# One transformer block with adaptive layer norm: shift matmuls first, reciprocals on ScalarE, last bias in the partial sums

## The chip, the core and the metric

The kernel runs on one core of one Trainium2 chip. A core has TensorE (PE), which multiplies matrices into PSUM; VectorE (DVE), ScalarE (ACT) and GpSimd (POOL), which work element by element; and SyncE (SP), whose queue here issues nearly all of the DMAs. ScalarE looks functions such as exponential or gelu up in tables that come in sets; a function from another set needs a table load first. The metric is the time of one execution on the device, in microseconds (us), lower is better. The time of a kernel is the median of its runs.

## The reference

A block over x of shape 8 x 1024 x 512, float32, with 16 heads of 32 columns and a hidden width of 2048. Weights, biases and the condition are inputs.

```python
mod = silu(condition) @ Wada + bada
sh_a, sc_a, gt_a, sh_m, sc_m, gt_m = split(mod, 6, axis=1)
xn = layernorm(x, g1, be1)
xm = xn * (1.0 + sc_a[:, None, :]) + sh_a[:, None, :]
x = x + gt_a[:, None, :] * attention(xm, Wqkv, Wproj, bproj)   # causal softmax
xn = layernorm(x, g2, be2)
xm = xn * (1.0 + sc_m[:, None, :]) + sh_m[:, None, :]
h = gelu(xm @ W1 + b1)
x = x + gt_m[:, None, :] * (h @ W2 + b2)
```

## The kernel before

The 8 x 1024 rows are cut into 16 blocks of 512 rows; a batch element has two. A block n goes through normalization, transposes, the three projections q, k and v, attention, the output projection, a second normalization, and the two matrix products around the gelu. The attention of block n runs while the projections of the next block and the products of the block before it are done, so that TensorE always has a second stream of work.

The linear products (helper `matmul`, L197) use TensorE as 128 rows x 32 columns: four matmuls stand side by side, one for each strip of 32 columns, and make one set. The attention works on 32 rows x 128 columns: four heads of 32 side by side. Transposes (L641) use all of 128 x 128. The kernel's own planner calls these "columns", "rows" and "whole" (`note_pe`) and charges 150 ns where one follows another. float32 products are run by the chip as two passes, so one matmul of the program is two records of the trace; bf16 takes one. Products of halves of matrices are combined in the manner of Strassen: sums of weight quarters are prepared once and kept in DRAM (`kept_up_S` and the like), and partial sums u1, u2, u3, u5, v3 are combined as they leave PSUM.

Attention has two kinds of tile, both in one PSUM buffer of four banks, `st`, which there is only once. A score tile (`scores_at_once`, L1391) has q as weights and k moving; VectorE adds the causal mask (L1405) and takes the maxima of rows (L1408). The maxima are split into three bf16 parts (`split_maxima`), turned into a row by TensorE (L1446) and copied out by ScalarE as `mrow` (L1452). A weight tile (`weights_T`, L1461) has k as weights (L1472) and then, in the same PSUM accumulation, a shift: minus ones times the row of maxima, in bf16 (L1484). ScalarE's exponential makes `pT` out of it (L1496), GpSimd cuts away what lies above the diagonal (L1501) and adds up the tiles of a group for the denominators (L1614), and `weigh` multiplies with v (L1524). A tile holds one part of 512 columns, or parts of 384 and 128, or two of 256.

`finish` (L1534) closes a group of four heads: TensorE sums the denominators (L1545), ScalarE copies them to `rec` (L1554) and the weighted sums to `top` (L1557), VectorE inverts `rec` in four pieces (L1563), which are put among its other work as jobs, and GpSimd multiplies (L1588).

`normalize` and `normalize_tile` take mean and variance on VectorE, the root on ScalarE (L563, L599) and its reciprocal on VectorE (L565, L604). `gates` makes the rows that scale the two residual sums: ga and gm, and gba and gbm, which are the gate times the bias (bproj, b2). `down` (L990) begins by adding gbm to the residual, a tile of 128 rows at a time (L1075), and copies its first partial sum u1 out of PSUM (L1079).

The order on every engine is written out by the program itself: a planner keeps a clock for each engine (`now`), the time at which each buffer is written and free (`written`, `left`), and costs that it notes with each instruction. `step_aside` (L1252) puts linear work ahead of an attention tile until the tile's inputs are due, the row of maxima among them; `work` takes the thread whose wait is the shortest; `either` (L150) gives an element-wise operation to VectorE or GpSimd, `copy_out` (L181) to VectorE or ScalarE. So an edit that changes a cost moves instructions elsewhere.

Of the kernel before, what the change touches and what calls it, by code (L numbers as in the profile page):

```python
# [22 lines left out]
def kernel(  # L23
# [259 lines left out]
    GATES = {"a": (2, bproj), "m": (5, b2)}  # L283
# [78 lines left out]
    vecs = [(g1, NC), (be1, NC), (g2, NC), (be2, NC), (bproj, NC), (b2, NC), (b1, NF), (bada, NMOD)]  # L362
# [7 lines left out]
    O_G1, O_BE1, O_G2, O_BE2, O_BPROJ, O_B2, O_B1, O_BADA = at  # L370
# [24 lines left out]
    nc.gpsimd.memset(minus_ones, -1.0)  # L395
    mcols = const.tile([P, NTT, P], BF16, tag="mcols", name="mcols")
# [7 lines left out]
    warm = const.tile([P, 1], F32, tag="warm", name="warm")  # L404
    nc.scalar.activation(warm, eps, AF.Sqrt)
    table[0] = "sqrt"
# [53 lines left out]
    def gates(kind):  # L460

        i, bias = GATES[kind]
        at = take(4)
        part = {kf: halves(j) for kf, j in zip(RAW, at)}
        b_gate = tmp.tile([P, D], F32, tag="y", name=f"b_gate_{kind}")[:B, :]
        b_out = tmp.tile([P, D], F32, tag="y", name=f"b_out_{kind}")[:B, :]
        nc.sync.dma_start(b_gate, bada[i * D : (i + 1) * D].unsqueeze(0).to_broadcast([B, D]))
        nc.sync.dma_start(b_out, bias.unsqueeze(0).to_broadcast([B, D]))
# [12 lines left out]
        release(*at)  # L481
        combine_out(b_gate, bank, ps, b_gate)
        nc.vector.tensor_tensor(b_out, b_out, b_gate, ALU.mult)
        note("DVE", 700, port=True)
        for name, row in ((f"g{kind}", b_gate), (f"gb{kind}", b_out)):
            kept_rows[name] = kept.tile([B, D], F32, tag=f"kept_{name}", name=f"kept_{name}")
            nc.sync.dma_start(kept_rows[name], row)

    def gate_broadcasts(b, kind):

        for name in (f"g{kind}", f"gb{kind}"):
# [52 lines left out]
    def normalize(tiles, key, sources):  # L544
# [17 lines left out]
        def root():  # L562
            nc.scalar.activation(rstd, mv[:, :, 1], AF.Sqrt, bias=eps)  # L563
# [26 lines left out]
    def normalize_tile(xt, key, t, source):  # L590
# [8 lines left out]
        nc.scalar.activation(rstd, mv[:, 1:2], AF.Sqrt, bias=eps)  # L599
        note_act(300, "sqrt", [("mv", key, t)], [("rstd", key, t)])  # L600
        written["hat", key, t] = NEVER

        def apply():
            nc.vector.reciprocal(rstd, rstd)  # L604
# [3 lines left out]
            nc.scalar.activation(xh, xt, AF.Identity, bias=offset, scale=rstd)  # L608
            note_act(800, None, [("rstd", key, t)], [("hat", key, t)])
            hats.setdefault(key, []).append(xh)  # L610
# [275 lines left out]
    def add_to(xt, other, reads, writes, op=ALU.add):  # L886
        either(xt, xt, other, op, [*reads, *writes], writes)
# [102 lines left out]
    def down(n, part):  # L990
# [81 lines left out]
        if part == 0:  # L1072
            yield [("g", n, 0), ("g", n, 1), "prepared"], []
            for i in range(NTT):
                add_to(residual[n][:, i, :], gate_rows["gbm"], [("row", "gbm")], [("xr", n, i)])  # L1075
# [3 lines left out]
            copy_out(got["u1"], bank, ps, [key("u1")])  # L1079
# [16 lines left out]
        elif part == 2:  # L1096
# [5 lines left out]
            settle(n, 0, 1, v3, key("v3"))  # L1102
        else:
# [357 lines left out]
    def weights_T(n, g, parts):  # L1461
# [6 lines left out]
        for k, c0, w, gg in parts:  # L1468
            kT = keys_of(n, k // NTT)
            for j in range(HPG):  # L1470
                r = slice(j * hd, (j + 1) * hd)
                nc.tensor.matmul(  # L1472
                    st[:, j, c0 : c0 + w],
                    kT[r, gg, ts(k % NTT, P)],
                    qT[r, gg, TB - w :],
                    start=(c0 == 0),
                    stop=False,
                    skip_group_check=True,
                )
        for k, c0, w, gg in parts:  # L1480
            row = m_rows[n, gg]
            for j in range(HPG):
                r = slice(j * hd, (j + 1) * hd)
                nc.tensor.matmul(  # L1484
                    st[:, j, c0 : c0 + w],
                    minus_ones[r, :],
                    row[r, TB - w :],
# [7 lines left out]
        used = parts[-1][1] + parts[-1][2]  # L1495
        nc.scalar.activation(pT[:, :, :used], st[:, :, :used], AF.Exp, scale=scale)  # L1496
# [37 lines left out]
    def finish(n, g):  # L1534
# [19 lines left out]
        nc.scalar.copy(rec, banks[bank])  # L1554
        note_act(585, None, [("l", bank)], [kr])
# [3 lines left out]
        part = TB // 4  # L1559

        def invert(i):
            some = rec[:, i * part : (i + 1) * part]
            nc.vector.reciprocal(some, some)  # L1563
            note("DVE", 920, [kr], [kr])

        if (n, g) == groups[-1]:
            for i in range(NTT):
                invert(i)
                some = slice(i * part, (i + 1) * part)
# [4 lines left out]
        if (n, g) == first_end:  # L1574
            for i in range(NTT):
                invert(i)
# [5 lines left out]
        def quotient():  # L1582
            invert(3)
            if n == NB - 1 and g == NC - 2:
                nc.vector.tensor_tensor(qTs[n][:, g, :], top, rec, ALU.mult)
                note("DVE", 700, [kr, "top"], [("att", n)], port=True)
            else:
                nc.gpsimd.tensor_tensor(qTs[n][:, g, :], top, rec, ALU.mult)  # L1588
                note("POOL", 1285, [kr, "top"], [("att", n)])
            if g == NC - 1:  # L1590
                written["attended", n] = 0.0
# [197 lines left out]
```

## Time and profile before

| | |
|---|---|
| median of 3 runs | 3600.94 us (3596.26 to 3602.02) |
| span of the profiled execution | 3594.6 us |
| TensorE busy | 98% |
| VectorE, ScalarE, GpSimd busy | 58%, 37%, 57% |
| mean granted clock of TensorE | 0.998 |

The profile is of one execution. Its page gives the busy time of each engine, the chain of waits that ended last, and the costliest groups of instructions. Views of the same trace list instructions in order of time, or group them by line, or list who waited for whom. In a group, `out<-in` are buffer names, then come partitions x elements and type, the count, the busy time, the mean length of one in ns, and the idle time before them with what ended it. "PE" is a matmul, "PEld" a load of weights. A line such as "PE sc L1391 <- DVE mx L1408: 8.1, 8, 1.1" says that TensorE waited for VectorE 8.1 us in total, 8 times, at most 1.1 us. A row of the windows view has the stretch, its length, then busy time and count of PE, PEld, DVE, ACT and POOL, the granted clock, the DMA engines' busy share and the GB/s that they moved.

### The profile page before, as it was taken

The numbers are of one execution on the slowest core, as the hardware profiler recorded it, in microseconds if no ns is written. First come the engines' busy times: TensorE is split into PE (matmuls) and PEld (weight loads), VectorE is DVE, ScalarE is ACT, GpSimd is POOL, SyncE is SP. The second block draws the span as 40 slices with busy tenths as digits, with TensorE's granted clock in tenths as the row PEclk, the third lists the DMA queues.
The fourth block names the chain that finished last, engine by engine and source line by source line (L and its number), as shares of the span: only waits on it lengthen the run. The fifth ranks groups of instructions, "written<-read, shape, count | busy, mean of one in ns | idle before, by whom it ended". The sixth has DMA issues, their size and how long they took to land.

```text
span 3594.6 us, 121150 instructions
## 1 busy us (share of the span) xinstructions
PE 3529.1 (98%) x54845; PEld 1774.2 (49%) x54845; DVE 2073.7 (58%) x2296; ACT 1328.0 (37%) x1395; POOL 2045.4 (57%) x2176
## 2 busy tenths in 40 slices
PE   8999999999999999999999999999999999999999
PEld 4444455445554555545555455444554545445445
DVE  6766675554746556465564655646557355564663
ACT  2335233352433524335242452424524244241421
POOL 3676746565465753666536665466654566544660
PEclk9999999999999999999999999999999999999999
DMA  6743233434343343433434334343343433335334
GB/s 201 235 150 90 81 116 104 121 104 130 110 125 104 105 132 113 142 93 99 128 112 137 98 99 128 109 131 104 98 131 104 139 99 105 121 95 154 90 113 137
DMA packets 307893, 430.34 MB, mean 120 GB/s; under 512 B 25900, under 2 KB 176236, under 8 KB 307380
## 3 DMA queue, kind: packets, MB, share of 16 engines
q1 hardware_dynamic: 307264, 422.56, 38.6%
q8 instruction: 432, 7.08, 0.8%
q14 instruction: 81, 0.66, 0.1%
q10 hardware_dynamic: 116, 0.03, 0.0%
HBM read 394.12 MB, written 28.38 MB: 118 GB/s over the span
## 4 chain that ended last, share of the span: by engine, by line
PE 89%; DVE 5%; POOL 3%; ACT 2%; issue 1%; DMA 1%; SPq 0%; ACTq 0%; DVEq 0%; POOLq 0%
PE bank L201 62%; PE sc L1391 8%; PE st L1472 8%; PE po L1524 7%; DVE mx L1408 2%; PE st L1484 2%; PE bank L1545 2%; PE bank L641 1%; POOL pT L1614 1%; ACT pT L1496 1%; DMA w<-in_L_cond_Wada_dram 1%; POOL xr L161 1%; DVE xr L158 0%; PE bank L1446 0%; DVE hT L1005 0%
## 5 line engine op out<-in xcount | busy, mean ns | idle before, releaser
L1614 POOL TENSOR_TENSOR pT<-pT,pT 128x256 f32<-128x256 f32 (+3 forms) x1254 | 1188.1, 983 | 430.6 <-PE po L1524 241.4
L1496 ACT ACTIVATE pT<-st 128x2048 f32<-128x2048 f32 x288 | 541.0, 1879 | 874.2 <-PE st L1484 832.5
L201 PE MATMUL bank<-w,hT 128*32 128x256 f32 x14336 | 807.5, 380 | 1.2 <-ACT rec L1554 0.9
L1408 DVE TENSOR_REDUCE mx<-sc 128x4 f32<-128x2048 f32 (+3 forms) x383 | 663.5, 1753 | 165.5 <-PE sc L1391 159.5
L201 PEld LDWEIGHTS bank<-w,hT 128*32 128x32 f32 x14336 | 454.8, 110 | 346.3 <-issue 54.2
L201 PE MATMUL bank<-xm_m,w 128*32 128x256 f32 x8192 | 496.0, 380 | 3.2 <-ACT xm_m L651 3.0
L201 PE MATMUL bank<-t_m,w 128*32 128x256 f32 x6144 | 388.7, 381 | 0.5 <-DVE t_m L660 0.5
L1501 POOL TENSOR_SCALAR_AFFINE_SELECT pT<-pT 128x512 f32<-128x512 f32 x256 | 165.4, 665 | 390.4 <-ACT pT L1496 390.4
L201 PEld LDWEIGHTS bank<-xm_m,w 128*32 128x32 f32 x8192 | 255.4, 110 | 225.9 <-issue 58.6
L1391 PE MATMUL sc<-kT,qT 32*128 32x512 f32 (+3 forms) x3064 | 328.0, 520 | 8.7 <-DVE mx L1408 8.1
L1472 PE MATMUL st<-qT,kT 32*128 32x512 f32 (+3 forms) x3072 | 329.9, 520 | 6.6 <-DVE mx L1408 5.3
L1405 DVE TENSOR_TENSOR sc<-sc,mask 128x1024 f32<-128x1024 f32 (+1 forms) x159 | 162.1, 1020 | 281.8 <-PE sc L1391 272.0
L1524 PE MATMUL po<-pT,v 128*32 128x512 f32 (+3 forms) x3072 | 304.2, 491 | 8.6 <-POOL pT L1501 8.6
L201 PEld LDWEIGHTS bank<-t_m,w 128*32 128x32 f32 x6144 | 188.3, 110 | 192.0 <-issue 75.5
L201 PE MATMUL bank<-xm_a,w 128*32 128x256 f32 x3968 | 240.3, 380 | 0.9 <-ACT p_k L188 0.9
L201 PE MATMUL bank<-w,qT 128*32 128x512 f32 x2048 | 237.4, 594 | 0.0
L1563 DVE RECIPROCAL rec<-rec 128x128 f32<-128x128 f32 x256 | 225.7, 920 | 11.3 <-ACT rec L1554 11.3
L1391 PEld LDWEIGHTS sc<-kT,qT 32*128 32x128 f32 x3064 | 129.6, 183 | 177.8 <-ACT pT L1496 78.9
L1472 PEld LDWEIGHTS st<-qT,kT 32*128 32x128 f32 x3072 | 129.8, 183 | 165.8 <-issue 72.6
L193 DVE TENSOR_TENSOR hT<-bank,u_u 128x512 f32<-128x512 f32 x192 | 129.0, 685 | 104.8 <-PE bank L201 104.1
L201 PE MATMUL bank<-t_a,w 128*32 128x256 f32 x2944 | 188.3, 380 | 0.0
L1427 POOL CAST mcols<-mx 128x16 bf16<-128x16 f32 x61 | 15.6, 256 | 289.9 <-DVE mx L1422 157.0
(206 smaller groups left out, 3608.6 us busy)
## 6 DMA issues: line engine op xcount, KB each, us to landing
w<-in_L_cond_W_dram SPq DMA_DIRECT2D x384, 256.0 KB
w<-kept_up_S SPq DMA_DIRECT2D x256, 256.0 KB
w<-kept_down_S SPq DMA_DIRECT2D x256, 256.0 KB
w<-kept_qkv_S SPq DMA_DIRECT2D x180, 256.0 KB
w<-in_L_cond_Wqkv_dram SPq DMA_DIRECT2D x147, 256.0 KB
hat<-in_x_dram SPq DMA_DIRECT2D x64, 256.0 KB
w<-in_L_cond_Wproj_dram SPq DMA_DIRECT2D x64, 256.0 KB
xr<-in_x_dram SPq DMA_DIRECT2D x64, 256.0 KB
```

The lines of the kernel that those rows point to most:

```text
L193: nc.vector.tensor_tensor(out, src, other, op)
L201: nc.tensor.matmul(ps[r, :], lhsT[:, r], rhs, start=start, stop=stop, skip_group_check=True)
L1391: nc.tensor.matmul(sc[:, j, c0 : c0 + w], qTs[n][r, gg, ts(qt, P)], keys_of(n, kh)[r, gg, :w], start=True, stop=True, skip_group_check=True,)
L1405: nc.vector.tensor_tensor(place, place, shape_of.to_broadcast(place.shape), ALU.add)
L1408: nc.vector.tensor_reduce(maxima[n, gg][:, kh, qt, :], sc[:, :, c0 : c0 + w], axis=AX.X, op=ALU.max)
L1472: nc.tensor.matmul(st[:, j, c0 : c0 + w], kT[r, gg, ts(k % NTT, P)], qT[r, gg, TB - w :], start=(c0 == 0), stop=False, skip_group_check=True,)
L1484: nc.tensor.matmul(st[:, j, c0 : c0 + w], minus_ones[r, :], row[r, TB - w :], start=False, stop=True, skip_group_check=True,)
L1496: nc.scalar.activation(pT[:, :, :used], st[:, :, :used], AF.Exp, scale=scale)
L1501: nc.gpsimd.affine_select(diagonal, diagonal, pattern=[[0, HPG], [1, P]], compare_op=ALU.is_ge, fill=0.0, base=0, channel_multiplier=-1,)
L1524: nc.tensor.matmul(po[r, TB - w :], v[:, k % NTT, g * P + j * hd : g * P + (j + 1) * hd], pT[:, j, c0 : c0 + w], start=(k == 0), stop=last ...
L1563: nc.vector.reciprocal(some, some)
L1614: nc.gpsimd.tensor_tensor(into, into, pT[:, j, c0 : c0 + w], ALU.add)
```

## The change

Three edits that go together.

In `weights_T` the shift matmuls of a tile stand ahead of its key matmuls; the shift now opens the accumulation and the keys close it.

Reciprocals become logarithm and exponential on ScalarE. The copy of the denominators out of PSUM is now a logarithm, and `invert` is an exponential of its negative, over all 512 columns at once (four pieces of 128 in the last group); it is no job any more but stands at once in `finish`. The multiplication may go to VectorE or GpSimd (`either`). The root of the variance and its reciprocal become exp(-0.5 ln(v + eps)). `exp_table` loads the set that has both functions; the set with the square root is no longer used.

The last bias b2 is no longer multiplied with the gate and added to the residual. Its two halves are loaded once, spread over all partitions (`b2_rows`: the low half, and the high half minus the low), the low half is added when u1 leaves PSUM, and the difference to u2 once v3 is made.

```diff
+    def exp_table():
+        if table[0] != "exp":
+            nc.scalar.preload_act_table_set("natural_log_exp_and_others")
...
-    GATES = {"a": (2, bproj), "m": (5, b2)}
+    GATES = {"a": (2, bproj), "m": (5, None)}
...
+    b2_rows = const.tile([P, 2, HB], F32, tag="b2_rows", name="b2_rows")
+    nc.scalar.dma_start(b2_rows.rearrange("p a n -> p (a n)"), b2.unsqueeze(0).to_broadcast([P, D]))
+    nc.gpsimd.tensor_tensor(b2_rows[:, 1, :], b2_rows[:, 1, :], b2_rows[:, 0, :], ALU.subtract)
...
         def root():
-            nc.scalar.activation(rstd, mv[:, :, 1], AF.Sqrt, bias=eps)
-            note_act(300, "sqrt", [("mv", key)], [("rstd", key)])
-            nc.vector.reciprocal(rstd, rstd)
+            exp_table()
+            nc.scalar.activation(rstd, mv[:, :, 1], AF.Ln, bias=eps)
+            nc.scalar.activation(rstd, rstd, AF.Exp, scale=-0.5)
+            note_act(500, "exp", [("mv", key)], [("rstd", key)])
...
-            for i in range(NTT):
-                add_to(residual[n][:, i, :], gate_rows["gbm"], [("row", "gbm")], [("xr", n, i)])
             combine(nc.vector, "B12", "B12", "B11")
             bank, ps = yield from product("B11")
             got["u1"] = stage("p1", "p1")
-            copy_out(got["u1"], bank, ps, [key("u1")])
+            b2_low = b2_rows[:, :1, :].to_broadcast([P, 2, HB])
+            combine_out(got["u1"], bank, ps, b2_low, [], [key("u1")])
...
             settle(n, 0, 1, v3, key("v3"))
+            add_to(u2, b2_rows[:, 1:, :].to_broadcast([P, 2, HB]), [], [key("u2")])
...
         for k, c0, w, gg in parts:
+            row = m_rows[n, gg]
+            for j in range(HPG):
+                r = slice(j * hd, (j + 1) * hd)
+                nc.tensor.matmul(
+                    st[:, j, c0 : c0 + w], minus_ones[r, :], row[r, TB - w :],
+                    start=(c0 == 0), stop=False, skip_group_check=True,
+                )
+        for k, c0, w, gg in parts:
             kT = keys_of(n, k // NTT)
...
-                    start=(c0 == 0),
-                    stop=False,
...
+                    start=False,
                     stop=True,
...
-        nc.scalar.copy(rec, banks[bank])
-        note_act(585, None, [("l", bank)], [kr])
+        exp_table()
+        nc.scalar.activation(rec, banks[bank], AF.Ln)
+        note_act(585, "exp", [("l", bank)], [kr])
...
-        def invert(i):
-            some = rec[:, i * part : (i + 1) * part]
-            nc.vector.reciprocal(some, some)
-            note("DVE", 920, [kr], [kr])
+        def invert(some=slice(0, TB)):
+            exp_table()
+            nc.scalar.activation(rec[:, some], rec[:, some], AF.Exp, scale=-1.0)
+            note_act(170 + 0.84 * (some.stop - some.start), "exp", [kr], [kr])
...
-        for i in range(3):
-            add_job(lambda i=i: invert(i), [kr], g == NC - 1)
-        add_job(quotient, [kr], g == NC - 1)
+        invert()
+        if n == NB - 1 and g == NC - 2:
+            nc.vector.tensor_tensor(qTs[n][:, g, :], top, rec, ALU.mult)
+            note("DVE", 700, [kr, "top"], [("att", n)], port=True)
+        else:
+            either(qTs[n][:, g, :], top, rec, ALU.mult, [kr, "top"], [("att", n)])
```

More of the change, by code (lines that the diff above doesn't have):

```diff
@@ L482, in gates @@
         combine_out(b_gate, bank, ps, b_gate)
-        nc.vector.tensor_tensor(b_out, b_out, b_gate, ALU.mult)
-        note("DVE", 700, port=True)
-        for name, row in ((f"g{kind}", b_gate), (f"gb{kind}", b_out)):
+        made = [(f"g{kind}", b_gate)]
+        if bias is not None:
+            nc.vector.tensor_tensor(b_out, b_out, b_gate, ALU.mult)
+            note("DVE", 700, port=True)
+            made.append((f"gb{kind}", b_out))
+        for name, row in made:
             kept_rows[name] = kept.tile([B, D], F32, tag=f"kept_{name}", name=f"kept_{name}")
@@ L489, in gate_broadcasts @@
     def gate_broadcasts(b, kind):
-        for name in (f"g{kind}", f"gb{kind}"):
+        for name in [name for name in (f"g{kind}", f"gb{kind}") if name in kept_rows]:
             row = rowp.tile([P, D], F32, tag=f"row{name}", name=f"row_{name}_{b}")
@@ L1580, in finish @@
             return
[L1582 to L1591, printed above, removed]
-        for i in range(3):
-            add_job(lambda i=i: invert(i), [kr], g == NC - 1)
-        add_job(quotient, [kr], g == NC - 1)
+        invert()
+        if n == NB - 1 and g == NC - 2:
[3 more added lines that the diff above has]
+            either(qTs[n][:, g, :], top, rec, ALU.mult, [kr, "top"], [("att", n)])
+        if g == NC - 1:
+            written["attended", n] = 0.0
     shared = {}
```

45 lines of the change are left out of this document (20 added, 25 removed).

## The prediction

> **What bounds the kernel now.** I read the page's head and its busy line first, then the stretches by window, then TensorE's own waits.
>
> ```profile
> span 3594.6 us, 121150 instructions
> PE 3529.1 (98%) x54845; PEld 1774.2 (49%) x54845; DVE 2073.7 (58%) x2296; ACT 1328.0 (37%) x1395; POOL 2045.4 (57%) x2176
> PE 89%; DVE 5%; POOL 3%; ACT 2%; issue 1%; DMA 1%; SPq 0%; ACTq 0%; DVEq 0%; POOLq 0%
> ```
> ```profile
> 0.00:30.00 30.00, 15.00 (x385) 11.68 (x389) 13.57 (x26) 8.27 (x12) 13.68 (x23) 1.00 0.83 269
> 450.00:3450.00 3000.00, 2975.39 (x46100) 1491.94 (x46096) 1703.73 (x1853) 1140.21 (x1192) 1742.12 (x1850) 1.00 0.38 115
> 3450.00:3595.00 145.00, 134.55 (x2284) 76.22 (x2276) 73.35 (x107) 26.59 (x39) 28.65 (x22) 0.99 0.43 129
> ```
> ```profile
> PE po L1524 <- POOL pT L1501: 8.6, 5, 2.1
> PE sc L1391 <- DVE mx L1408: 8.1, 8, 1.1
> PE bank L201 <- DMA w<-in_L_cond_Wada_dram: 6.6, 6, 2.3
> PE st L1472 <- DVE mx L1408: 5.3, 6, 1.8
> PE bank L1545 <- POOL pT L1614: 3.8, 1, 3.8
> PE bank L641 <- ACT xh_m L608: 3.3, 3, 2.5
> PE bank L201 <- ACT xm_m L651: 3.0, 7, 0.4
> ```
>
> TensorE is the bound: it idles 3594.6 - 3529.1 = 65.5 us, only 24.6 of them in the 3000 us from 450 to 3450. VectorE, GpSimd and ScalarE are busy 37 to 58%, and what they do reaches the end only through the waits listed last. So an edit counts where it changes TensorE's instruction stream, or one of those waits. But a busy TensorE is not a streaming one, so next I looked at what one attention tile costs it.
>
> ```profile
> 1341.59 1.14 PE L1391 MATMUL sc<-kT,qT 32*128 32x512 f32 x8
> 1342.66 3.23 PE L201 MATMUL bank<-xm_a,w 128*32 128x256 f32 x56
> 1345.70 0.61 PE L201 MATMUL bank<-t_a,w 128*32 128x256 f32 x8
> 1346.25 1.14 PE L1472 MATMUL st<-qT,kT 32*128 32x512 f32 x8
> 1347.21 0.39 PE L1484 MATMUL st<-mrow,minus_ones 32*128 32x512 bf16 x4
> 1347.54 1.07 PE L1524 MATMUL po<-pT,v 128*32 128x384 f32 x16
> ...
> 3472.50 13.92 PE L201 MATMUL bank<-w,qT 128*32 128x512 f32 x128
> ```
>
> These are rows of the timeline: start, length, then what. Four records run side by side as one set; an fp32 product is two passes, so two sets. The last row has 32 sets of 512 columns: less the 0.59 us that the last one takes to drain, 13.33 / 31 = 0.43 us a set. The 56 records at 1342.66 give 3.04 / 14 = 0.217 us for a set of 256, so a one-pass bf16 set of 512 should take 0.216. Now the tile at 1346.25: its two key sets should take 0.86 us but the shift starts 0.96 later, so 0.10 is lost; the shift set should take 0.22 but the next work starts 0.33 later, so 0.11 is lost. The score tile at 1341.59 loses both, 1.07 against 0.86. The 0.11 is the change of form (32 rows x 128 columns to 128 x 32); the same stands on the way in (0.55 for two sets of 256 at 1345.70). The 0.10 is a weight load that nothing covers, since it comes right behind a change of form. Which load it is matters:
>
> ```profile
> L1472 PEld LDWEIGHTS st<-qT,kT 32*128 32x128 f32 x3072 | 129.8, 183 | 165.8 <-issue 72.6 <-DVE mx L1408 37.7 <-PE bank L201 22.2
> L1484 PEld LDWEIGHTS <-minus_ones 32*128 32x128 bf16 x1536 | 43.5, 93 | 46.6 <-issue 42.9
> L1446 PEld LDWEIGHTS <-mcols 128*32 128x32 bf16 x1024 | 20.1, 97 | 15.4 <-POOL mcols L1430 4.0 <-issue 2.7 <-DVE mcols L1430 0.7
> ```
> ```profile
> 1339.10 0.41 PE L1446 MATMUL bank<-ident_b,mcols 128*32 128x128 bf16 x16
> 1339.33 1.46 PE L1524 MATMUL po<-pT,v 128*32 128x512 f32 x16
> ...
> 1142.00 0.41 PE L1446 MATMUL bank<-ident_b,mcols 128*32 128x128 bf16 x16
> 1142.23 1.04 PE L1524 MATMUL po<-pT,v 128*32 128x512 f32 x8
> ```
>
> The key load takes 183 ns, the shift's only 93. What a 93 ns load shows behind a change of form is not in this trace, but its neighbour is: the maxima's bf16 load (97 ns) came behind a change of form at 1339.10 and behind none at 1142.00, and both took 0.23 us. So it shows about 0.01 us or less.
>
> **The change part by part.** *Shift first.* Behind the change of form comes the 93 ns load, not the 183 ns one, and the key load runs under the shift set. A 512 tile gets 0.01 + 0.216 + 0.86 + 0.11, about 1.20 for 1.29: 0.094 saved. A tile of two 256 parts also: its second shift set (0.108) covers the 0.104 load. A tile of 384 and 128 ends its shifts with a set of 0.054, so 0.05 of the key load shows again and 0.044 is saved. The counts, at 8 records a 512 tile, 8 of 384 or 16 of 256:
>
> ```profile
> L1472 PE MATMUL st<-qT,kT 32*128 32x512 f32 x1536 | 219.8, 639 | 6.6 <-DVE mx L1408 5.3 <-ACT pT L1496 0.3
> L1472 PE MATMUL st<-qT,kT 32*128 32x384 f32 x512 | 59.4, 533 | 0.0
> L1472 PE MATMUL st<-qT,kT 32*128 32x256 f32 x512 | 36.7, 400 | 0.0
> ```
>
> 192 x 0.094 + 32 x 0.094 + 64 x 0.044 = 23.8 us saved. Bounds: none if the bf16 load shows 0.104 after all; 26 if it shows nothing. I take 23.8, since 93 ns is nearest to 97.
>
> The shift now needs its row of maxima at the tile's start, not 0.5 to 1.1 us into it. Behind a shift that waits stands all of TensorE's queue. The closest kind of place:
>
> ```profile
> 2073.09 0.58 ACT L1452 CAST mrow<-bank 128x512 bf16<-128x512 f32 x1
> 2074.08 1.15 PE L1472 MATMUL st<-qT,kT 32*128 32x256 f32 x16
> ```
>
> The row is written at 2073.67, 0.41 before the tile begins: the planner already held the tile for it. I cost it at nothing; a row later by more than that is a rival.
>
> *The new order.* The planner re-laid TensorE's stream. I counted changes of form in the two compiled orders: 1251 before, 1300 after; transposes (L641) now come in 93 runs, not 54, often singly between two sets. 49 x 0.11 = 5.4 us more, and 39 more first transposes whose load shows between 0 and 0.10; taking 0.05 each gives 2.0. Together +7.4, bounds +5.4 and +9.3.
>
> *Waits.* One wait repeats every two blocks:
>
> ```profile
> 957.91 0.64 PE L201 MATMUL bank<-xm_m,w 128*32 128x256 f32 x8
> 958.36 1.91 PE L201 MATMUL bank<-t_m,w 128*32 128x256 f32 x32
> 958.84 2.29 DVE L1408 TENSOR_REDUCE mx<-sc 128x4 f32<-128x2048 f32 x1
> 961.27 1.15 PE L1391 MATMUL sc<-kT,qT 32*128 32x384 f32 x16 [1.00 <-DVE mx L1408]
> ```
>
> Between the two score tiles stand 10 sets (40 records, 20 instructions) while VectorE masks and reduces. The changed order has 32 instructions there, six more sets of 0.216 = 1.3 us, over the 1.00 waited. Seven places: -7. The xm_m waits (7, 3.0 us) may go or stay: -1. The 39 more runs of transposes may each meet a normalized tile not yet there: none, up to one wait of 1.0 us (3.3 us in 3, above) in each of seven periods: +3.
>
> *Start.* The last bias is now loaded as 256 KB across all partitions, ahead of work that waits for DMA; at 269 GB/s that is 0.95 us. I take +1, bounds 0 and 1. SP issues 10 loads and stores fewer in the whole run, none of which TensorE waited for.
>
> *Reciprocals, tables, bias.*
>
> ```profile
> L1563 DVE RECIPROCAL rec<-rec 128x128 f32<-128x128 f32 x256 | 225.7, 920 | 11.3 <-ACT rec L1554 11.3
> L563 ACT ACT_TABLE_LOAD x29 | 37.2, 1283 | 0.4
> L947 ACT ACTIVATE hT<-hT,cols 128x512 f32<-128x512 f32 x256 | 165.2, 712 | 27.9 <-DVE hT L193 27.2
> L161 POOL TENSOR_TENSOR xr<-xr,row_gbm 128x512 f32<-128x512 f32 x43 | 76.7, 1813 | 0.0
> ```
>
> VectorE loses 225.7 us. ScalarE's logarithm replaces a copy of the same size; the exponential adds 64 x 0.712, about 46 us, while table loads fall from 177 to 117 in the compiled orders, 60 x 1.283 = 77 us. GpSimd loses 76.7 us of bias adds and gets 16 smaller ones. All of it lies beside TensorE, on engines with 42 to 63% idle, so I cost it at nothing beyond the waits above. Without that cover, 46 us of exponentials on ScalarE is the most it could cost; the most it could bring is DVE's and POOL's part of the waits, 8.6 + 8.1 + 5.3 + 3.8 = 25.8, of which I have counted 7.
>
> *Sum.* -23.8 + 7.4 - 7 - 1 + 3 + 1 = -20.4 us: the profiled 3594.6 becomes 3574.2. The median of the runs, 3600.9, lies 6.3 above its profile; the prediction is 3600.9 - 20.4 = 3580.5.
>
> **The rivals.** *The gain is hidden.* The shift's load shows 0.104 like the key load: nothing saved, and the rest of the sum gives +3.4, 3604.3. Against it stand the 93 and 97 ns. The Trainium skill's page "TensorE: Matmul & The Clock Gate", section "LDWEIGHTS (loading the stationary operand)", speaks for it: a load takes its columns / 1.2 GHz, so 107 ns for 128 columns of either type, and it agrees with the 0.10 of the key load. Its section on Fast Weight Load excepts 128 columns that are not FP32; the 93 ns here side with that exception.
>
> *Slower: the row comes late.* Where ScalarE writes the row of maxima more than 0.41 us later against TensorE than at 2073.67, the shift holds the whole queue. With logarithm and exponential queued before it, one row could be 1.0 us later: 64 x 0.59 = 38, 3580.5 + 38 = 3618. For it: ScalarE works in order. Against: ScalarE is 63% idle and the planner accounts the row at the tile's start in both orders.
>
> *Slower: the turn from bf16 to fp32 inside a tile drains like a change of form.* 0.11 + 0.10 for each of 288 tiles is 60 us: 3580.5 + 60 = 3640.5. Against: at 1142.23 fp32 follows bf16 with nothing lost.
>
> *More waits go.* With VectorE 11% freer all 25.8 us go, 18.8 more than counted: 3562.
>
> **How the numbers follow.** Forecast 0.69, hidden gain 0.10, late row 0.05, draining turn 0.04, more waits gone 0.12. About 0.2%, 7.2 us, is what a measurement here can tell from no change: faster means below 3593.7. Faster has 0.80: the last rival, and the forecast but for 0.01 at its upper edge. That 0.01 and the hidden gain are the same, 0.11; the two slower rivals have 0.09. The range goes down to the last rival and up to where half of the shift's gain (11.9) and two thirds of the seven waits' (4.7) fail to come: 3562 to 3597.
>
> **What would show it.** Right: a 512 tile with the shift first has its keys 0.23 us behind the shift, and the next form 0.97 behind the keys; the wait of L1391's successor on the 384 tile is gone; table loads 117; VectorE about 225 us less busy, with no trace in the time. Wrong: 0.32 between shift and keys; the shift's line among TensorE's waits on the row; or idle of TensorE well above 65 us.

## The result, and the profile after

The changed kernel takes 3553.0 us (median of 4 runs, 3550.3 to 3554.3) where the kernel before took 3600.0 beside it (4 runs, 3596.3 to 3602.0). The ratio is 0.9872, 95% interval 0.9858 to 0.9885: 47 us less, by the interval 41 to 51. The forecast was 3580.5 with a range from 3562; the direction was right, and the gain was more than twice the 20.4 us of the sum.

The page of the changed kernel: the span, the busy time of each engine, and the shares of the chain that ended last.

```profile
span 3548.6 us, 120656 instructions
PE 3507.2 (99%) x54845; PEld 1766.5 (50%) x54845; DVE 1884.8 (53%) x2041; ACT 1271.7 (36%) x1406; POOL 1960.7 (55%) x2116
PE 94%; POOL 2%; ACT 2%; DVE 1%; issue 1%; DMA 1%; SPq 0%; DVEq 0%; ACTq 0%; POOLq 0%
```

The span fell by 46.0 us. TensorE is busy 21.9 us less (3529.1 to 3507.2) and idle 24.1 us less (65.5 to 41.4). The sum had 16.4 and 4: the busy part was forecast nearly, the idle part was not. The windows say where the idle time went.

```profile
0.00:30.00 30.00, 14.92 (x353) 10.93 (x357) 12.36 (x25) 8.03 (x11) 14.15 (x23) 1.00 0.86 277
450.00:3404.00 2954.00, 2946.41 (x45892) 1478.83 (x45885) 1530.09 (x1639) 1086.13 (x1189) 1664.78 (x1788) 1.00 0.38 115
3404.00:3549.00 145.00, 134.61 (x2292) 77.24 (x2280) 70.90 (x96) 25.07 (x45) 27.75 (x20) 0.98 0.43 129
```

The first 30 us and the last 145 are as before (15.1 and 10.4 us of idle, before 15.0 and 10.45). The long middle idles 7.6 us where it idled 24.6. So most of the idle time that went, 17.0 us, lay in the steady part, and 7.2 us lay between 30 and 450. TensorE's waits show which waits went:

```profile
PE bank L653 <- DVE xm_m L657: 3.8, 7, 0.5
...
PE po L1537 <- POOL pT L1514: 2.9, 2, 2.2
...
PE sc L1403 <- ACT pT L1509: 1.6, 1, 1.6
PE st L1484 <- DVE mx L1420: 1.4, 3, 0.9
PE bank L205 <- DMA w<-in_L_cond_Wada_dram: 1.2, 4, 0.4
PE sc L1403 <- DVE mx L1420: 1.1, 2, 0.8
```

Against the rows of before: the weighted sum on GpSimd's cut of `pT` 2.9 for 8.6 (now L1537 and L1514), scores on the maxima 1.1 for 8.1, the weight tile on the maxima 1.4 for 5.3; the denominators' 3.8 on GpSimd's sum and the 3.0 on xm_m are gone, and a new wait of transposes on xm_m has 3.8.

From the timeline of the changed kernel (start, length, what), first the two diagonal score tiles that had the wait of 1.00 us at 961.27 between them, then a weight tile of 512:

```profile
940.81 1.14 PE L1403 MATMUL sc<-kT,qT 32*128 32x512 f32 x8
941.88 1.93 PE L205 MATMUL bank<-t_m,w 128*32 128x256 f32 x32
943.63 1.91 PE L205 MATMUL bank<-xm_m,w 128*32 128x256 f32 x32
945.48 1.15 PE L1403 MATMUL sc<-kT,qT 32*128 32x384 f32 x16
...
1524.14 0.40 PE L1484 MATMUL st<-mrow,minus_ones 32*128 32x512 bf16 x4
...
1524.37 1.03 PE L1496 MATMUL st<-qT,kT 32*128 32x512 f32 x8
...
1525.33 1.50 PE L1537 MATMUL po<-pT,v 128*32 128x512 f32 x16
```

Between the score tiles stand 64 records of linear work (32 matmuls) where 40 stood, and the 384 tile carries no idle mark. In the weight tile the keys start 0.23 us behind the shift and the next form 0.96 behind the keys: 1.19 us for a tile of 512 where the prediction had about 1.20, and 1.29 before.

ScalarE's groups by line, with the table loads:

```profile
L145 ACT ACT_TABLE_LOAD x58 | 74.4, 1283 | 1.0
L959 ACT ACT_TABLE_LOAD x58 | 74.4, 1283 | 6.4 <-DVE hT L197 5.4
L1576 ACT ACTIVATE rec<-rec 128x512 f32<-128x512 f32 (+1 forms) x67 | 41.7, 627 | 0.0
L1568 ACT ACTIVATE rec<-bank 128x512 f32<-128x512 f32 x64 | 38.0, 594 | 108.4 <-PE bank L1558 108.3
```

With one load of the start that makes the 117 loads that were forecast, and 80 us of logarithm and exponential for 225.7 us of reciprocals.

### The profile page after: what moved, and what is told of

Read it like the earlier page. It is cut to its first block, busy times and chain, and to the rows that moved or that the text cites. A ratio compares the mean times of both kernels' runs of the same rounds, so it can differ in the third digit from the quotient of the medians.

```text
span 3548.6 us, 120656 instructions
## 1 busy us (share of the span) xinstructions
PE 3507.2 (99%) x54845; PEld 1766.5 (50%) x54845; DVE 1884.8 (53%) x2041; ACT 1271.7 (36%) x1406; POOL 1960.7 (55%) x2116
## 3 DMA queue, kind: packets, MB, share of 16 engines
q1 hardware_dynamic: 306080, 420.43, 38.9%
## 4 chain that ended last, share of the span: by engine, by line
PE 94%; POOL 2%; ACT 2%; DVE 1%; issue 1%; DMA 1%; SPq 0%; DVEq 0%; ACTq 0%; POOLq 0%
PE bank L205 65%; PE sc L1403 8%; PE po L1537 7%; PE st L1496 7%; PE st L1484 2%; PE bank L653 2%; PE bank L1558 2%; POOL pT L1620 1%; ACT pT L1509 1%; PE bank L1458 0%; DVE mx L1420 0%; POOL hT L165 0%; ACT hT L959 0%; DMA hat<-in_x_dram 0%; DVE sc L1417 0%
## 5 line engine op out<-in xcount | busy, mean ns | idle before, releaser
L1514 POOL TENSOR_SCALAR_AFFINE_SELECT pT<-pT 128x512 f32<-128x512 f32 x256 | 170.4, 684 | 430.5 <-ACT pT L1509 429.1
L1537 PE MATMUL po<-pT,v 128*32 128x512 f32 (+3 forms) x3072 | 304.7, 491 | 2.9 <-POOL pT L1514 2.9
L1496 PE MATMUL st<-qT,kT 32*128 32x512 f32 (+3 forms) x3072 | 300.0, 486 | 0.0
L165 POOL TENSOR_TENSOR qT<-top,rec 128x512 f32<-128x512 f32 x61 | 78.5, 1286 | 295.4 <-ACT rec L1576 291.8
L205 PEld LDWEIGHTS bank<-xm_a,w 128*32 128x32 f32 x3968 | 120.8, 110 | 108.5 <-issue 34.5
L959 ACT ACTIVATE hT<-hT,cols 128x512 f32<-128x512 f32 x256 | 164.3, 711 | 24.3 <-DVE hT L197 23.6
```

The lines of the kernel that those rows point to most:

```text
L165: nc.gpsimd.tensor_tensor(out, a, b, op)
L205: nc.tensor.matmul(ps[r, :], lhsT[:, r], rhs, start=start, stop=stop, skip_group_check=True)
L959: nc.scalar.activation(hT[:, i, :], hT[:, i, :], AF.Gelu, bias=cols[:, O_B1 + f : O_B1 + f + 1])
L1496: nc.tensor.matmul(st[:, j, c0 : c0 + w], kT[r, gg, ts(k % NTT, P)], qT[r, gg, TB - w :], start=False, stop=True, skip_group_check=True,)
L1514: nc.gpsimd.affine_select(diagonal, diagonal, pattern=[[0, HPG], [1, P]], compare_op=ALU.is_ge, fill=0.0, base=0, channel_multiplier=-1,)
L1537: nc.tensor.matmul(po[r, TB - w :], v[:, k % NTT, g * P + j * hd : g * P + (j + 1) * hd], pT[:, j, c0 : c0 + w], start=(k == 0), stop=last ...
```

## The experiments

The question was the 24 us of idle time. Three theories: VectorE and GpSimd are freer, and what they held up comes sooner (A, relief); the planner, which sees cheaper operations, laid TensorE's stream anew (B, order); the shift first itself takes waits away (C). "Relief" is meant with the order of all instructions held; "stream" is the order in which TensorE gets its matmuls. For each kernel below, TensorE's time is split in three: idle (span less busy); "lost", the time lost to a lower clock, which is (1 - granted clock) times busy time, summed over windows of 4 us; and "work", busy less lost. These three are of the one profiled execution of each kernel, the ratio is of all its runs. Differences are in us.

| kernel | ratio to before, 95% | idle | lost | work |
|---|---|---|---|---|
| before | 1 | 65.5 | 4.4 | 3524.7 |
| after | 0.9872 [0.9858, 0.9885] | 41.4 | 1.6 | 3505.6 |
| e1_shift | 0.9934 [0.9922, 0.9946] | 66.9 | 6.2 | 3502.3 |
| e2_recip | 0.9962 [0.9948, 0.9975] | 48.4 | 6.0 | 3528.2 |
| e3_bias | 0.9967 [0.9954, 0.9979] | 55.1 | 5.9 | 3523.8 |
| e4_no_shift | 0.9928 [0.9916, 0.9941] | 38.9 | 3.1 | 3529.9 |
| r1_relief | 0.9995 [0.9986, 1.0004] | 62.3 | 6.7 | 3525.9 |
| r2_load_back | 0.9952 [0.9940, 0.9964] | 59.2 | 14.2 | 3508.9 |
| r3_pool_relief | 0.9973 [0.9961, 0.9984] | 56.8 | 4.9 | 3524.3 |
| r4_plan_only | 1.0039 [1.0026, 1.0052] | 68.8 | 6.1 | 3532.3 |
| r5_plan_relief | 1.0013 [1.0004, 1.0022] | 62.8 | 11.1 | 3529.6 |
| e6_division | 0.9975 [0.9966, 0.9984] | 54.7 | 9.4 | 3528.6 |
| e5_roots | 0.9980 [0.9971, 0.9989] | 56.8 | 7.5 | 3524.8 |
| x1b_at_once | 1.0247 [1.0233, 1.0261] | 118.3 | 19.1 | 3546.2 |
| x2_as_jobs | 0.9959 [0.9945, 0.9972] | 50.4 | 4.9 | 3523.5 |
| b_switch100 | 1.0077 [1.0063, 1.0091] | 75.1 | 10.4 | 3534.6 |
| v_switch100 | 0.9913 [0.9900, 0.9927] | 59.1 | 7.1 | 3499.4 |
| b_switch220 | 1.0017 [1.0008, 1.0026] | 66.6 | 6.9 | 3531.7 |
| v_switch220 | 0.9903 [0.9890, 0.9917] | 51.0 | 6.2 | 3506.2 |
| v_jobs | 0.9885 [0.9872, 0.9899] | 50.4 | 4.8 | 3501.3 |

### The three parts alone

The shift first alone:

```diff
 before.py, weights_T
+        for k, c0, w, gg in parts:   # shift: start=(c0 == 0), stop=False
         for k, c0, w, gg in parts:   # keys: start=False, stop=True
-        for k, c0, w, gg in parts:   # shift
```

> The kernel before with the shift matmuls first in each weight tile, and nothing else changed. The changed kernel's trace has a 512 tile at 1184 ns for 1286, so 192 + 32 tiles x about 0.09 to 0.10 and 64 x 0.05 are about 25 us of TensorE's work. Theory A (the rest of the gain is VectorE's and GpSimd's relief) and theory B (the rest is the new order that the planner makes with the cheaper costs): about -25 us, near 3575 us beside 3600, with TensorE's idle at 65 +- 5 us as before. Theory C (the shift first itself takes waits away, since a tile then ends sooner and what follows meets its inputs): -35 us or more, idle 55 us or less.

Measured: 3575.5 us beside 3599.1, a gain of 24 us. Idle stayed at 66.9 and work fell by 22.4. Theory C falls: the shift first saves the loads and takes no wait away.

The reciprocals alone (the edits of `root`, `normalize_tile`, `finish` and `exp_table`):

```diff
-            nc.vector.reciprocal(some, some)
+            nc.scalar.activation(rec[:, some], rec[:, some], AF.Exp, scale=-1.0)
```

> The kernel before with logarithm and exponential on ScalarE in place of the reciprocals, and the one table set; shift and last bias as before. Theories A and B: the waits of TensorE on VectorE's maxima (8.1 and 5.3 us) go almost entirely here, idle falls by 10 to 20 us, time about 3580 to 3590 us. Theory C: nothing to gain from it beyond 5 us, 3595 to 3600 us.

Measured: 3584.5 us, 14 us less by the ratio. Idle fell by 17.1 us, and work rose by 3.5. The scores' wait on the maxima went from 8.1 to 2.0 us, the cut's from 8.6 to 2.5, and the denominators' 3.8 went; the weight tile's wait on the maxima did not go (6.6 for 5.3), against the expectation.

The last bias alone:

```diff
-                add_to(residual[n][:, i, :], gate_rows["gbm"], [("row", "gbm")], [("xr", n, i)])
+            combine_out(got["u1"], bank, ps, b2_low, [], [key("u1")])
+            add_to(u2, b2_rows[:, 1:, :].to_broadcast([P, 2, HB]), [], [key("u2")])
```

> The kernel before with the last bias in the partial sums alone. GpSimd loses 76.7 us. Theories A and B: the waits on GpSimd's pT (8.6 and 3.8 us) shrink, idle falls by 3 to 8 us, time about 3592 to 3597 us. Theory C: within 3 us of before.

Measured: 3587.3 us, 12 us less, and idle 10.4 less: more than any of the theories expected. The cut's wait fell from 8.6 to 0.8 and the denominators' 3.8 went; the scores' 8.1 stayed as it was.

Reciprocals and bias together, without the shift:

```diff
 after.py, weights_T
-        for k, c0, w, gg in parts:   # shift
         for k, c0, w, gg in parts:   # keys: start=(c0 == 0), stop=False
+        for k, c0, w, gg in parts:   # shift: start=False, stop=True
```

> The changed kernel with the shift put back behind the keys, so reciprocals and bias together. Theories A and B: the changed kernel's 3553 and 25.6 us of exposed loads and drains, about 3578 to 3581 us, TensorE's idle at 41 to 45 us. Theory C: 3590 us or more, idle 50 us or more.

Measured: 3573.0 us, 26 us less, idle 38.9. That is 5 us under the expectation: the shift's place is worth 20 us here, and the expectation had put 25.6. The parts add up: 24 + 14 + 12 = 50 alone, 47 together. The gain that the sum had missed lies in the two parts that it had costed at nothing, and what they bring is idle time.

### The bias: relief, with the order held still

In the kernel before, all 64 adds of the last bias to the residual are cut to one column, 43 on GpSimd and 21 on VectorE. `either` still decides and notes by the full size, so no instruction moves on any engine.

```diff
-                add_to(residual[n][:, i, :], gate_rows["gbm"], ...)
+                either(xt, xt, row, ALU.add, [...], [...], slice(0, 1))
```

> The kernel before, in its own order on every engine, with each add of the last bias to the residual on one column of 512 only; so the last bias is left out for the other columns. GpSimd loses some 70 us and no instruction moves. Relief of GpSimd as the cause of the bias edit's 12 us: TensorE's waits on GpSimd's pT (8.6 and 3.8 us) fall below 4 us together, time 8 to 12 us below before, 3588 to 3592. The planner's new order as its cause: the waits stay, within 3 us of before.

Measured: 3589.1 us beside 3599.7, a gain of 10 us (6 to 14 by the interval), idle 8.7 less. So most of the bias' 12 us comes without a new order. The timeline of the kernel before shows the mechanism at one of three places in the steady part:

```profile
2558.65 6.21 POOL L161 TENSOR_TENSOR xr<-xr,row_gbm 128x512 f32<-128x512 f32 x3
...
2562.81 0.64 PE L201 MATMUL bank<-t_m,w 128*32 128x256 f32 x8
2564.82 0.63 POOL L1501 TENSOR_SCALAR_AFFINE_SELECT pT<-pT 128x512 f32<-128x512 f32 x1
...
2565.50 1.06 PE L1524 MATMUL po<-pT,v 128*32 128x512 f32 x8 [2.06 <-POOL pT L1501]
```

Three bias adds, 6.21 us, stand in GpSimd's queue ahead of the cut. TensorE has done its linear work at 2563.45 and waits 2.06 us for a cut that takes 0.63. With the adds on one column the same rows of r3_pool_relief read:

```profile
2556.13 2.45 POOL L163 TENSOR_TENSOR xr<-xr,row_gbm 128x1 f32<-128x1 f32 x3
2558.62 0.63 POOL L1504 TENSOR_SCALAR_AFFINE_SELECT pT<-pT 128x512 f32<-128x512 f32 x1
```

The cut comes 3.7 us sooner behind the adds' start, and the cut's wait falls from 8.6 in five places to 3.2 in two; the three that went are those of the steady part, 5.3 us.

The relief has a second path, through VectorE. The weight tile's wait on the maxima fell from 5.3 to 2.4 us with the same edit. At one of the three places that went, first before, then in r3_pool_relief:

```profile
2329.17 3.39 DVE L158 TENSOR_TENSOR xr<-xr,row_gbm 128x512 f32<-128x512 f32 x2
2332.49 4.53 DVE L1005 TENSOR_TENSOR hT<-hT 128x1024 f32<-128x1024 f32 x2
...
2337.54 2.27 DVE L1408 TENSOR_REDUCE mx<-sc 128x4 f32<-128x2048 f32 x1
...
2339.87 1.14 PE L1472 MATMUL st<-qT,kT 32*128 32x512 f32 x8 [1.74 <-DVE mx L1408]
```
```profile
2328.46 1.23 DVE L160 TENSOR_TENSOR xr<-xr,row_gbm 128x1 f32<-128x1 f32 x2
...
2329.62 2.35 DVE L1007 TENSOR_TENSOR hT<-hT 128x1024 f32<-128x1024 f32 x2
```

Two bias adds of VectorE stand ahead of the maxima, and the pair of sums behind them takes 4.53 us before and 2.35 here. The denominators' wait (3.7) stayed, against the expectation: no bias add stands in GpSimd's queue in the 9 us before that wait ends, from 402.40 to 411.58 us of the kernel before. It went in e3_bias, where the order is another; by what, is not shown.

### The reciprocals: not relief alone, and not the order alone

The kernel before, with each reciprocal on one column; no other engine's instructions move:

```diff
-            nc.vector.reciprocal(some, some)
+            nc.vector.reciprocal(some[:, :1], some[:, :1])
             note("DVE", 920, [kr], [kr])
```

> The kernel before, in its own order on every engine, with each reciprocal on one column of 128 only; so the division by the denominators is left out for the other columns. VectorE loses about 200 of its 225.7 us, and no instruction of another engine moves. Theory A (relief): idle of TensorE falls by 13 to 20 us, 3580 to 3587 us beside 3600. Theory B (the new order): the waits stay, since the maxima's own 2.3 us reduction and the work laid beside it are the same; within 5 us of before.

Measured: 3596.1 us, ratio 0.9995 [0.9986, 1.0004], although VectorE is busy 198 us less. Theory A, with the order as it was, falls for the reciprocals. Its timeline shows why, at one of the seven places:

```profile
957.08 0.64 PE L201 MATMUL bank<-xm_m,w 128*32 128x256 f32 x8
957.27 0.70 DVE L1405 TENSOR_TENSOR sc<-sc,mask 128x512 f32<-128x512 f32 x1 [0.96 <-PE sc L1391]
957.53 1.91 PE L201 MATMUL bank<-t_m,w 128*32 128x256 f32 x32
958.00 2.29 DVE L1408 TENSOR_REDUCE mx<-sc 128x4 f32<-128x2048 f32 x1
...
960.44 1.15 PE L1391 MATMUL sc<-kT,qT 32*128 32x384 f32 x16 [1.00 <-DVE mx L1408]
```

VectorE had been waiting for the scores when they came (0.96). Mask and maxima take 0.70 + 2.29 us and TensorE has only ten sets of work in that time. No reciprocal was in the way here, so its going frees nothing.

The other side: the changed kernel, its order unchanged, with VectorE's load put back on an unused tile.

```diff
         invert()
+        for i in range(4):
+            piece_of = spare[:, ts(i, P)]
+            add_job(lambda piece_of=piece_of: nc.vector.reciprocal(piece_of, piece_of), [kr], g == NC - 1)
```

> The changed kernel with four reciprocals of 128 x 128 per group on an unused tile, put in as jobs that the planner doesn't account, so its order of all else stands and VectorE has some 225 us of load back. Theory A: waits on VectorE come back, idle rises from 41 to 55 us or more, 3565 to 3575 us. Theory B: within 5 us of the changed kernel's 3553.

Measured: 3582.8 us, 30 us above the changed kernel, more than theory A asked for, and B is out as well. The load comes back as something else than the old waits. The timeline at one of seven such places, and windows there and at another:

```profile
2223.86 1.91 PE L205 MATMUL bank<-xm_a,w 128*32 128x256 f32 x32
...
2224.08 3.35 DVE L1599 RECIPROCAL spare<-spare 128x128 f32<-128x128 f32 x4
2227.35 1.22 DVE L197 TENSOR_TENSOR kT<-bank,u_k 128x512 f32<-128x512 f32 x2
...
2228.03 2.48 PE L205 MATMUL bank<-t_a,w 128*32 128x256 f32 x28 [2.26 <-DVE kT L197]
```
```profile
2226.00:2228.00 2.00, 0.00 (x0) 0.00 (x0) 2.00 (x4) 0.00 (x0) 1.14 (x3) 1.00 0.53 167
2228.00:2229.00 1.00, 0.97 (x17) 0.56 (x21) 0.57 (x1) 0.00 (x0) 0.00 (x0) 0.92 0.08 26
2229.00:2232.00 3.00, 3.00 (x28) 1.06 (x20) 0.69 (x1) 0.00 (x0) 0.00 (x0) 0.50 0.00 0
...
906.00:908.00 2.00, 0.00 (x0) 0.00 (x0) 2.00 (x4) 0.00 (x0) 1.32 (x3) 1.00 0.62 181
908.00:912.00 4.00, 3.78 (x56) 1.92 (x56) 1.46 (x3) 0.78 (x2) 0.00 (x0) 1.00 0.24 51
```

Four reciprocals in a row hold up the copy of kT out of PSUM, TensorE waits 2.26 us for the bank, seven times (15.8 us in all), and in five of the seven the clock is at 0.50 for some 3.4 us behind the wait. The first three windows are of one of the five, the last two of one of the two others. Idle is up by 17.8 us, the loss by 12.6. The loss is not the same each time: one of the five executions, at a mean clock of 0.999, took 3574.4 us, the other four, at 0.995 or 0.996, 3582.4 to 3584.0. The kernel tells what an unplanned burst on VectorE costs; that the planned load costs as much is not shown by it.

Next, what the planner believes was parted from what VectorE does. In the kernel before, the note of a reciprocal goes from 920 to 0 ns, once with the work in full and once with one column:

```diff
-            note("DVE", 920, [kr], [kr])
+            note("DVE", 0, [kr], [kr])
```

> The kernel before with every reciprocal done in full, but accounted by the planner at 0 ns for 920. VectorE's work is that of before; only the order is that of a planner that believes VectorE free of it (32 matmuls for 20 stand between the diagonal score tiles). If the order alone took the waits: the wait of scores on the maxima falls from 8.1 to 2 us or less, and the time is 8 us or more below before, 3585 to 3592. If order and relief are both needed: the reciprocals now come in bursts that nobody planned for, other waits on VectorE come in place, and the time is at or above before, 3597 to 3620.

> The same order as r4_plan_only on every engine, with each reciprocal on one column of 128 only (the division is left out for the other columns). If the order alone took the waits: within 3 us of r4_plan_only. If both are needed: 8 to 15 us below before, 3584 to 3592, while r4_plan_only is not.

Measured: 3614.2 and 3603.5 us. Both streams have 32 matmuls between the diagonal score tiles, and the scores' wait went from 8.1 to 3.4 in the first and out of the list in the second. Neither is faster than before: other waits came (in the first on kT 4.0, on the maxima's columns `mcols` 3.5 and 2.2, for 1.6 before), and work rose by 7.6 and 4.9 us. The second came out as neither of its two expectations had it. A new order alone, as far as this one stands for it, is not the cause of the 14 us; nor does relief in this order bring a gain against before. The 11 us between the two are what the relief is worth once the planner counts on it.

Then the edit was cut in two, and the division's place moved.

```diff
 e6_division: finish as after; roots, table set as before
 e5_roots: root, normalize_tile, table set as after; finish as before
 x1b_at_once: before, with
-            add_job(lambda i=i: invert(i), [kr], g == NC - 1)
+            invert(i)
 x2_as_jobs: e2_recip, with
-        invert()
+        add_job(quotient, [kr], g == NC - 1)   # exponential and product
```

> The kernel before with the softmax's division by logarithm and exponential alone; the norms keep root and reciprocal with their table set. If VectorE's 225.7 us and their place in the plan carry the 14 us of the reciprocals' edit: 10 to 14 us below before, 3585 to 3590. If the norms and the one table set carry it: within 4 us of before.

> The kernel before with the norms by logarithm and exponential and the one table set alone; the softmax's division stays as reciprocals on VectorE. The reciprocals' edit gave 13.7 us and the division alone 8.4: if the two halves add up, 4 to 7 us below before, 3593 to 3596. If the norms only help together with the division: within 3 us of before.

> The kernel before with three of a group's four reciprocals issued on VectorE at once when the group is closed, and not as jobs laid later; accounted and done in full. If the gain of the division's edit is its earlier place alone, whatever engine does it: 6 to 12 us below before, 3588 to 3594. If it is that VectorE's queue no longer holds 0.92 us pieces near the maxima: no gain, 3600 to 3615, with more waits on VectorE.

> The kernel with the reciprocals' edit alone (3584.5 us), but the exponential and the product of a group laid later as one job, as the reciprocals were. If the gain is the work that left VectorE: within 3 us of 3584.5. If it is the place at the group's end: back to 3593 to 3600.

Measured: the division alone 3591.3 us, 9 less by the ratio (a little short of what was expected); the norms with one table set 3591.0, 7 less (a little more than was expected); together 14. Reciprocals on VectorE at once: 3686.1, 89 us more and far beyond what was expected: idle rose by 52.8 us, work by 21.5, the loss by 14.7. The weight tile's wait on the maxima went from 5.3 to 14.9 us, but most of the new waits are others, and they were not taken apart. The exponential laid later as a job: 3582.0, as good as at once. So the division's gain does not hang on its place at the group's end. That it goes with the work that leaves VectorE fits, but is not shown, since each of these kernels has an order of its own. It can't be the reason for the norms' 7 us: in e5_roots VectorE is as busy as before (2078.2 us for 2073.7), and what fell is ScalarE's busy time, from 1328.0 to 1251.3.

### How much is the luck of a stream

One constant of the planner, its charge for a change of form, was moved in both kernels.

```diff
-    SYNC, PIPE, SWITCH, TABLE = 100, 250, 150, 1283
+    SYNC, PIPE, SWITCH, TABLE = 100, 250, 100, 1283   # and 220
```

> The changed kernel with the planner charging 100 ns for 150 where one form of matmul follows another. Its stream has 1238 changes of form for 1300, but 20 matmuls stand between the diagonal score tiles again for 32. If the form changes weigh more: 62 x 0.11 to 0.21 us = 7 to 13 us, less at most 7 us of waits that come back, so 3541 to 3553. If the planner's stream as a whole decides by its waits: 3553 to 3560.

> The kernel before with the planner charging 100 ns for a change of form instead of 150; its pair is v_switch100, the changed kernel with the same charge, 3566.2 us. If the change is worth 46 us whatever stream the planner lays: 3566 + 46 = 3612, within 5 us. If part of the 46 us is the luck of two streams: a pair that differs by under 36 or over 56 us.

> The changed kernel with a charge of 220 ns, near what a change of form and the weight load behind it were seen to cost (0.11 + 0.10 us). If that charge makes the better stream: 3545 to 3552. If the streams differ by chance: 3550 to 3566. Against its pair as written there.

> The kernel before with a charge of 220 ns; its pair is v_switch220. If the change is worth 46 us in any stream: 41 to 51 us above its pair. If luck is in it: under 36 or over 56 us above. Its own time by the spread seen so far: 3587 to 3613.

Measured: 3566.2 and 3622.5 us at 100 ns, 3563.4 and 3606.8 at 220. The pairs differ by 56 and 43 us, by 47 at 150: the change is worth 43 to 56 us in three streams (41 to 59 by the ratios), and idle falls by 16, 16 and 24 us. The 56 lies at the edge that the expectation had set for luck. A single kernel moves by 7 to 23 us with the constant alone, so a difference of 10 us between two streams needs no other cause; the 14 us of the reciprocals and their halves of 9 and 7 lie within that spread too. If the shift's 24 and the bias' 12 hold in every stream, which was not run, 7 to 20 us of each pair are left for the reciprocals. At 100 ns the changed kernel came out slower than either of its expectations: it has less work (3499.4, 1238 changes of form) and more idle time (59.1): scores wait 7.0 us on the maxima again, with 20 matmuls between the tiles.

The last one tried for a better version, the changed kernel with the division as a job, as in x2_as_jobs:

```diff
-        invert()
+        add_job(quotient, [kr], g == NC - 1)   # exponential and product
```

> The changed kernel with the exponential and the product of a group laid later as one job, as in x2_as_jobs, which stood 2.4 us below its own pair. 1246 changes of form for 1300, 24 matmuls between the diagonal score tiles for 32. If the fewer changes of form decide: 3545 to 3551, the fastest here. If the 24 matmuls bring the waits back (7 x 0.5 us) and the rest is chance: 3551 to 3560.

Measured: 3557.3 us, 4 above the changed kernel. Work fell by 4.3 us and idle rose by 9.0. No version tried beats the changed kernel.

## Why the prediction was wrong

By its own steps:

- *Shift first, -23.8*: right. Alone it gives 24 us (19 to 28 by the interval), in work, with the intervals 0.23 and 0.96 in the tile. Both rivals that spoke against it fall: the bf16 load doesn't show 0.10, and the turn from bf16 to fp32 costs nothing.
- *The row of maxima, nothing*: right. The shift waits 1.4 us in three places, where the keys waited 5.3 in six.
- *The new order's changes of form, +7.4*: right in kind and a little large. Without the shift, work rose by 5.2 us (e4_no_shift).
- *The seven waits, -7*, and *xm_m, -1 and +3*: right for the seven, 8.1 us became 1.1. On xm_m +2 was a little much: seven waits of 3.0 us in all became seven of 3.8.
- *Start, +1*: idle in the first 30 us rose by 0.1. The start's wait for Wada differs by several us between traces of one order (6.6 before, 3.2 in r1_relief), so the fall from 6.6 to 1.2 in the changed kernel isn't put down to the change.
- *Reciprocals, tables, bias: "All of it lies beside TensorE, on engines with 42 to 63% idle, so I cost it at nothing beyond the waits above"*. This is the step that failed. The share of idle time of an engine says nothing of the order in its queue. GpSimd is idle 43% of the span, and three bias adds of 6.21 us still stood ahead of a cut that TensorE waited for. The step also left out the 21 bias adds on VectorE (21.6 us in the trace of before), two of which stood ahead of maxima that a weight tile waited for. The row was in the prediction (po on GpSimd's pT, 8.6, 5 times), and the question what stood ahead of that cut was not asked; its answer was in the trace of before. The relief was worth 10 us with the order held still, 12 with the edit as a whole.
- The same step missed the reciprocals' part. The prediction's terms for their new order, forms and waits together, sum to about +2; measured were -14 alone. What is shown: relief in the old order gives nothing, cheaper costs in the plan without relief lose 14 us, two different places of the division give the same gain, and the norms alone give 7 and the division alone 9. So the cause of these 14 us stays open, and with it why a stream that counts on free reciprocals and has nearly free ones (r5_plan_relief) gains nothing, when one with the division on ScalarE (e6_division) gains 9. The spread between streams that one constant makes is as large.
- The rival *more waits go*, 3562 with a chance of 0.12, came nearest, and the time went below it. Of its 25.8 us, 20.4 went (8.6 + 8.1 + 5.3 + 3.8 to 2.9 + 1.1 + 1.4), besides 5.4 of the start's DMA wait. Its reason, a freer VectorE, is not what the runs show: r1_relief has that alone and gains nothing, and the bias adds were for the most part GpSimd's. It also lacked the clock: the loss fell from 4.4 to 1.6 us between the two traces, which may be chance, since r1_relief, in the order of before, lost 6.7.

VectorE is 189 us less busy and not 225: the operations that `either` gave it take 222.6 us for 190.6, and copies with an add 492.7 for 480.6.

In sum: -19.1 of work (forecast -16.4), -24.1 of idle (forecast -4), -2.8 of lost clock (not in the forecast) are the 46.0 us between the two spans.

## What to carry to other kernels

An edit on an engine that isn't the bound is costed at the places where the bound engine waits for that engine: take each such wait, read from the timeline what stood ahead of the awaited instruction in its queue, and ask whether the edit removes it. Where an automatic planner lays the order, hold the order still and shrink the work (and the other way round) to part relief from order, and move one constant of the planner in both kernels to learn how much of a small gain is luck.

## What the runs showed of the hardware

A wait of TensorE can cost more than its length. Behind the seven waits of 2.26 us in r2_load_back the granted clock stood at 0.50 for some 3.4 us five times, a further 1.7 us each, and twice it stayed at 1.00. Nor does the length of the wait alone decide: in the kernel before the 2.06 us at 2563.45 left it at 1.00, and it fell behind 1.70 us of waiting at 606.40, as that kernel's windows show.

```profile
2564.00:2566.00 2.00, 0.50 (x8) 0.20 (x12) 1.48 (x2) 1.99 (x2) 1.92 (x3) 1.00 0.45 131
2566.00:2568.00 2.00, 2.00 (x40) 1.10 (x36) 0.00 (x0) 2.00 (x4) 2.00 (x2) 1.00 0.00 0
...
606.00:608.00 2.00, 0.40 (x4) 0.16 (x2) 1.97 (x3) 2.00 (x3) 2.00 (x3) 1.00 0.10 34
...
609.00:611.00 2.00, 1.85 (x32) 1.08 (x34) 1.90 (x2) 1.29 (x2) 2.00 (x2) 0.56 0.03 8
```

The Trainium skill, page "TensorE: Matmul & The Clock Gate", section "Part 1: The HAM clock gate (the "warmup" mystery)", has the clock halved after an idle window of about 3.4 us that runs freely, and back after as long a busy one. The length of the slow stretches agrees, and that two of seven equal waits left the clock alone fits a window that runs freely. But waits shorter than that window, 2.26 and 1.70 us, sufficed here.

The same operation can take very different times on GpSimd and on VectorE. Three adds of 128 x 1 on GpSimd took 2.45 us at 2556.13 in r3_pool_relief, but over all 43 of them the median is 195 ns (179 to 1239; spans on GpSimd are rough):

```profile
L163 POOL TENSOR_TENSOR xr<-xr,row_gbm x43: 179/195/1239, 307.4 to 3488.9; 128x1 f32<-128x1 f32 x43
L160 DVE TENSOR_TENSOR xr<-xr,row_gbm x21: 144/149/1164, 305.7 to 3387.2; 128x1 f32<-128x1 f32 x21
```

At 2556.13 VectorE ran two sums of 128 x 1024 at the same time (2556.18, 2.35 us). The other way round, such a pair took 4.53 us beside GpSimd's work at 2332.49 of the kernel before, and 2.35 at the same place of r3_pool_relief. That the two engines hold each other up would fit; no run here tests it.
